# Moving sums, late shared experts and the router's logits in a fused cross-attention and mixture-of-experts kernel

## The chip, the cores and the metric

The kernel runs on one core of a Trainium2 chip. The core has TensorE (PE in the profile, with its weight loads as PEld), VectorE (DVE), ScalarE (ACT), GpSimd (POOL) and SyncE (SP), and 16 DMA engines that all queues share. Each engine executes its instructions in the order in which the program issued them. The metric is device time in microseconds (us); less is better. Matmul results land in PSUM, of which this kernel uses two banks for attention scores and six that everything else takes in turn.

## The reference, cut to what matters

```python
# x (64, 128, 128), ctx_768 (64, 77, 96), all float32; 16 heads of 64
x = x + xattn(layernorm(x), ctx_768, w_q, w_kv, w_out, b_out)
# mixture of experts on h = layernorm(x), 8192 tokens of width 128
logits = h @ router_w.T                    # 8 experts
idx    = top_k(softmax(logits), 2)         # the two best
gate   = logits at idx                     # weighted by the logits themselves
for e in range(8):
    moe += gate[:, e] * ((silu(h @ w1[e].T) * (h @ w3[e].T)) @ w2[e].T)   # inner width 176
moe += (silu(h @ sw1.T) * (h @ sw3.T)) @ sw2.T                             # shared expert
x = x + moe
```

## The kernel before, in words

**Attention.** The 64 batches are 16 groups of four. A group has eight units (batch `b`, half of the heads `t`), so there are 128 units. In the loop at L1099 one unit issues, in this order: the scores of the unit two ahead (`ps`, L365, then on DVE the maximum L374 and the subtraction L376), every second unit the output product of a batch (`py`, L444), the steps of plan slot 2k, the transposes of its own weights (`pa`, L434, copied by ACT at L437), the exponentials of the unit two ahead (ACT, L380), the value products (`pv`, L417, copied by ACT at L422), the steps of plan slot 2k+1, and the weights of the unit two ahead (DVE sum L387 and reciprocal L389, POOL products L395 to L399). The score tile `ps` has one buffer, so the next unit's scores wait until DVE's L376 has read the last ones.

**The plan.** `at(when, step)` writes an order by hand: slot `when` is half a unit, group `g` of attention begins at slot 16g. Slot k always carries one step of `keys` (`pk` L348, copied by ACT at L355) as its first step. After group `g` of attention ends, its routing runs at slots p = 16(g+1) onwards: statistics at p, normalising at p+1, transpose at p+3, logits at p+4 (four matmuls of 8 columns, `pl` L553, then DVE L557 to L561 and ACT's Exp L562), the first choice at p+5 (`choose`, L578 to L572), the second at p+6, `place` at p+8, eight scatters by POOL (`send`, L643) from p+9. The shared expert has its two wide products at p+11 (`gated`), its rest (the inner columns 128 to 175, `gated_rest`: product L654, ACT tanh L518, DVE L520 and L521) at p+12 and its down product at p+14. Attention's own statistics for the next group are at slot 16g+2.

**Experts.** Groups are routed in three sets of 9, 5 and 2. When a set is placed, `tables` works out which expert each block of 128 rows belongs to. Four blocks are a `Quad`: load (SP, L746), copy of weights (ACT and DVE, L769), transpose L775, `first` and `rest` (L782), `down` (L794, L795), ACT's scaling to `y` (L801), and four scatters by POOL (`answer`, L805). The quads of set 0 and two of set 1 run inside attention. `Combine` brings a group's answers back: SP loads the parked sum (L835) and the answers `ya` (L838, 512 KB), DVE adds twice (L847), SP stores (L851).

**The ending.** After attention, `ending` runs passes over 19 jobs: ten quads of set 1 (KEPT), three shared experts (LATE: groups 13, 14, 15), six quads of set 2. In pass k it issues the load of job k+2, the steps listed under k in `ahead_of`, then first(k), transpose(k+1), rest(k), down(k-1), answer(k-1). The jobs stand in the order five quads, three shared experts, eleven quads. The sums of set 0 are all in the plan, from slot 239 to 259, and so partly behind attention's last slot 255 but ahead of the ending, which is at slot 260.

Of the kernel before, what the change touches and what calls it, by code (L numbers as in the profile page):

```python
# [8 lines left out]
F32 = mybir.dt.float32  # L9
# [6 lines left out]
B, NQ, D = 64, 128, 128  # L16
# [9 lines left out]
NT = 10  # L26
# [4 lines left out]
W1, W3, WR, W2F, W2R, WALL = 0, 128, 256, 256 + HI, 384 + HI, 512 + HI  # L31
G = 4
# [4 lines left out]
LATE = 3  # L37

# [17 lines left out]
NAT = 2  # L56
NHR = 2
# [9 lines left out]
def xattn_moe_kernel(  # L67
# [12 lines left out]
    rwT: bass.AP,  # L80
# [72 lines left out]
    rw_sb = const.tile([D, E], F32, name="rw_sb")  # L153
# [4 lines left out]
    nc.sync.dma_start(out=rw_sb, in_=rwT)  # L158
# [33 lines left out]

    hrs = [const.tile([128, T], F32, name=f"hr_{i}") for i in range(NHR)]

# [86 lines left out]
    class Norm:  # L281
# [5 lines left out]
        def stats(self):  # L287
            st = small.tile([128, G, 6], F32, tag="st", name=f"st_{self.name}")
            self.mv = small.tile([128, G, 2], F32, tag="mv", name=f"mv_{self.name}")
# [4 lines left out]
            ve = small.tile([128, G], F32, tag="ve", name=f"ve_{self.name}")  # L294
            nc.vector.tensor_scalar(ve, self.mv[:, :, 1], EPS, None, ALU.add)
            self.rs = small.tile([128, G], F32, tag="rs", name=f"rs_{self.name}")
# [189 lines left out]
    def gated(name, up, silu=False, n=T):  # L486
# [6 lines left out]
        h = ffn.tile([128, T], F32, tag="h", name=f"h_{name}", bufs=3)  # L493
# [12 lines left out]
    def gated_rest(name, up, silu=False, n=T):  # L506
# [4 lines left out]
        hr = hrs[hr_no[0] % NHR]  # L511
        hr_no[0] += 1
# [11 lines left out]
    class Router:  # L524
# [25 lines left out]
        def logits(self):  # L550
            pl = bank(f"pl_{self.g}")
            for b in range(G):
                nc.tensor.matmul(  # L553
                    pl[:, b * E : (b + 1) * E], self.x2T[:, b * NQ : (b + 1) * NQ], rw_sb, start=True, stop=True
                )
            self.lg = lg = self.t3("lg")
            nc.vector.tensor_copy(lg.rearrange("p b e -> p (b e)"), pl[:, : G * E])  # L557
# [37 lines left out]
        def place(self):  # L595
# [22 lines left out]
            for src, to, by in ((at, pos, 1.0), (self.lg, self.pay[:, :, :, D + 1].rearrange("p c b -> p c b"), 0.5)):  # L618
                m = small.tile([128, 2, G, E], F32, tag="picked", name=f"picked_{g}", bufs=2)
# [39 lines left out]
        def shared_rest(self, silu=False):  # L659
            self.hr = gated_rest(f"s{self.g}", self.up, silu)  # L660
# [72 lines left out]
    class Quad:  # L733
# [56 lines left out]
        def down(self):  # L790
# [8 lines left out]
            self.y = ffn.tile([128, QUAD, D], F32, tag="y", name=f"y_{self.name}")  # L799
# [102 lines left out]
    for g in range(NG):  # L902
# [4 lines left out]
        if g + 1 < NG:  # L907
# [3 lines left out]
            at(p + 2, lambda g=g: stats(g + 1))  # L911
# [21 lines left out]
    for g in range(NG - 1):  # L933
        p = 16 * (g + 1)
        routing(g, p, (0, "stats"), (1, "normed"), (3, "transpose"), (4, "logits"), (5, "choose"), (6, "choose_second"))
    for st in sets:
        for g in range(st.start, min(st.start + st.n, NG - 1)):
            p = 16 * (g + 1)
            routing(g, p, (8, "place"))
            if g < NG - LATE:  # L940
                routing(g, p, (11, "shared_up"), (12, "shared_rest"), (14, "shared_down"), (17, "park"))
# [12 lines left out]
    for st, after in zip(sets, sets[1:]):  # L954
# [25 lines left out]
    def job_of(quad, n):  # L980
# [15 lines left out]
    def shared(g):  # L996
# [8 lines left out]

    late = [shared(g) for g in range(NG - LATE, NG)]
    sent_by = KEPT // 2
    jobs = blocks[:sent_by] + late + blocks[sent_by:]
    passes = len(jobs)

    first_of_last = KEPT + LATE
# [19 lines left out]
    for j in range(before_last.n):  # L1031
        c = Combine(before_last, j)
        k = first_of_last + 2 + j
# [163 lines left out]
```

## Time and profile before

| what | value |
|---|---|
| time, median of 3 runs | 988.45 us (987.61 to 989.02) |
| the profiled execution: its own time | 985.48 us |
| the profiled execution: span of the profile | 983.8 us |
| granted TensorE clock, mean | 0.978 |
| PE busy | 924.1 us (94%) |
| PEld, DVE, ACT, POOL busy | 771.5, 671.4, 652.8, 517.4 us |
| HBM read, written | 48.18 MB, 36.33 MB |

The span is what the profile covers; the execution's own time is 1.7 us more. Attention without quads runs from about 20 to 465 us, attention with quads to about 851 us, the ending to 984 us. Busy time is an average over these stages, so the stages are read one by one.

### The profile page before, as it was taken

To read this page: it belongs to the slowest core of one execution; us is meant where nothing else is said; L and a number is where in the kernel's file an instruction comes from. 1 tells how busy PE (TensorE), PEld (TensorE's weight loads), DVE (VectorE), ACT (ScalarE), POOL (GpSimd) and SP (SyncE) were. 2 spreads that over 40 slices of the span, in tenths; PEclk is the share of its full clock that TensorE was granted. 3 is DMA by queue.
4 is the path that set the end of the run, shared out by engine and by line. 5 is a ranking of instruction groups with operands and counts; after the bars stand their busy time and mean duration, and the time that the engine had idled before them with its cause. 6 is when DMAs were issued, how large, how long until landed. Compare 5 with 4: busy or idle time off the path is not lost.

```text
span 983.8 us, 18867 instructions
## 1 busy us (share of the span) xinstructions
PE 924.1 (94%) x6123; PEld 771.5 (78%) x6123; DVE 671.4 (68%) x1751; ACT 652.8 (66%) x1420; POOL 517.4 (53%) x688
## 2 busy tenths in 40 slices
PE   8999999999999999999999999999999987779990
PEld 7887877787787878777888788888888876678980
DVE  4566776676667767768687677776676779566642
ACT  5776767676767667675776767667767665556760
POOL 3244563636364544636367375574474564437673
PEclk9999999999999999999999999999999999879996
DMA  6222212212222222122322221223121135723475
GB/s 179 70 62 71 67 41 81 68 57 71 72 71 65 75 73 65 44 86 80 89 70 76 83 82 55 59 69 99 57 85 49 37 121 169 228 66 98 109 212 174
DMA packets 80882, 85.76 MB, mean 87 GB/s; under 512 B 11328, under 2 KB 62912, under 8 KB 80784
## 3 DMA queue, kind: packets, MB, share of 16 engines
q1 hardware_dynamic: 65920, 56.09, 20.8%
q0 software_dynamic: 8864, 18.30, 5.6%
q10 hardware_dynamic: 6000, 10.16, 2.9%
q8 instruction: 49, 0.80, 0.3%
q14 instruction: 49, 0.40, 0.1%
HBM read 48.18 MB, written 36.33 MB: 86 GB/s over the span
## 4 chain that ended last, share of the span: by engine, by line
PE 69%; DVE 10%; ACT 9%; DMA 5%; issue 4%; SPq 2%; POOL 1%; ACTq 0%; DVEq 0%; POOLq 0%
PE py L444 13%; PE ps L365 11%; PE pk L348 11%; PE pv L417 8%; PE pa L434 5%; PE p L782 4%; PE p_s L654 3%; PE pn L454 2%; PE ph L782 2%; PE pq L794 2%; PE pq L795 2%; DMA answers<-y,to 2%; PE pf L667 1%; PE pf L666 1%; DMA out_dram<-yx 1%
## 5 line engine op out<-in xcount | busy, mean ns | idle before, releaser
L348 PEld LDWEIGHTS pk<-cT,wkq_sb 96*128 96x128 f32 x1024 | 157.8, 189 | 70.0 <-issue 42.8
L805 POOL DMA_INDIRECT answers<-y,to x149 | 146.4, 983 | 89.7 <-issue 44.7
L355 ACT COPY kx<-pk 128x308 f32<-128x308 f32 x256 | 104.5, 417 | 128.5 <-PE pk L348 123.2
L348 PE MATMUL pk<-cT,wkq_sb 96*128 96x154 f32 x1024 | 175.0, 294 | 1.0 <-ACT wkq_sb L265 0.7
L444 PEld LDWEIGHTS py<-vo,aT 128*128 128x128 f32 x1280 | 155.7, 194 | 15.8 <-ACT vo L422 5.2
L365 PE MATMUL ps<-kx,xgT 128*128 128x308 f32 x512 | 156.8, 426 | 9.7 <-DVE sc L376 9.1
L444 PE MATMUL py<-vo,aT 128*128 128x128 f32 x1280 | 157.9, 278 | 4.3 <-ACT vo L422 3.9
L643 POOL DMA_INDIRECT sent<-pay,row x128 | 126.3, 987 | 61.5 <-DVE part L633 27.6
L397 POOL TENSOR_TENSOR at<-sc,ri 128x512 f32<-128x512 f32 x64 | 67.2, 1050 | 170.9 <-DVE ri L389 117.6
L422 ACT COPY vo<-pv 64x512 f32<-64x512 f32 x256 | 147.3, 575 | 2.1 <-ACT vn L462 0.4
L417 PE MATMUL pv<-wvo_sb,cM 96*128 96x512 f32 x256 | 131.1, 594 | 1.0 <-DVE hr L521 0.8
L387 DVE TENSOR_REDUCE sm<-sc 128x8 f32<-128x616 f32 x128 | 101.1, 790 | 39.6 <-ACT sc L380 38.8
L380 ACT ACTIVATE sc<-sc,rs_a 128x616 f32<-128x616 f32 x128 | 105.0, 820 | 26.9 <-DVE sc L376 17.9
L365 PEld LDWEIGHTS ps<-kx,xgT 128*128 128x128 f32 x512 | 88.9, 189 | 38.6 <-issue 9.4
L437 ACT COPY aT<-pa 128x512 f32<-128x512 f32 (+1 forms) x256 | 96.2, 430 | 33.9 <-PE pa L434 29.2
L395 POOL TENSOR_TENSOR at<-sc,ri 128x256 f32<-128x256 f32 x128 | 77.1, 625 | 79.1 <-DVE ri L389 25.3
L376 DVE TENSOR_TENSOR sc<-ps,mx 128x616 f32<-128x616 f32 x128 | 102.4, 800 | 12.5 <-POOL at L399 0.4
L374 DVE TENSOR_REDUCE mx<-ps 128x8 f32<-128x616 f32 x128 | 98.3, 768 | 7.6 <-PE ps L365 6.4
L434 PE MATMUL pa<-ident,at 128*128 128x128 f32 x640 | 92.2, 275 | 0.0
L782 PE MATMUL p<-xT,w 128*128 128x128 f32 x596 | 77.0, 284 | 10.8 <-ACT xT L777 5.5
L434 PEld LDWEIGHTS pa<-ident,at 128*128 128x128 f32 x640 | 75.7, 143 | 11.2 <-issue 10.7
L782 PEld LDWEIGHTS p<-xT,w 128*128 128x128 f32 x596 | 72.8, 198 | 14.6 <-ACT xT L777 8.0
(152 smaller groups left out, 1405.6 us busy)
## 6 DMA issues: line engine op xcount, KB each, us to landing
xb<-sent SPq DMA_DIRECT2D x149, 65.0 KB
last_values<-vn ACTq DMA_DIRECT2D x32, 256.0 KB
vo<-last_values SPq DMA_DIRECT2D x64, 128.0 KB
ya<-answers SPq DMA_DIRECT2D x15, 512.0 KB
xgT<-in_xT_dram SPq DMA_DIRECT2D x16, 256.0 KB
xg<-in_x_dram SPq DMA_DIRECT2D x16, 256.0 KB
parked<-x SPq DMA_DIRECT2D x14, 256.0 KB
yx<-parked SPq DMA_DIRECT2D x14, 256.0 KB
```

The lines of the kernel that those rows point to most:

```text
L348: nc.tensor.matmul(pk[:, k].rearrange("p (b k) -> p b k", k=NKV), wkq_sb[:, 2 * i + k, :], self.cT[:, 2 * p : 2 * (p + 1), :], start=True, ...
L355: nc.scalar.copy(self.kx[p][:, hs, :], pk)
L365: nc.tensor.matmul(ps[:, r, : 4 * NKV].rearrange("p (j k) -> p j k", k=NKV), self.xgT[:, ts], self.kx[p][:, h : h + 4, ks], start=True, st ...
L376: nc.vector.tensor_tensor(at, sc, over_keys(mx), ALU.subtract)
L380: nc.scalar.activation(at, at, AF.Exp, scale=self.norm.rs[:, b : b + 1])
L417: nc.tensor.matmul(pv, self.cM[:, p, KM * r : KM * (r + 2)], wvo_sb[:, h : h + 4, :], start=True, stop=True)
L422: nc.scalar.copy(self.vo[b][rows, 4 * t : 4 * (t + 1), :], pv[rows].rearrange("p (m d) -> p m d", d=D))
L434: nc.tensor.transpose(pa[:, j * NQ : (j + 1) * NQ], keys[:, c : c + 128], ident)
L444: nc.tensor.matmul(py[:, :D], aT[:, m, :], vo[:, m, :], start=(m == 0), stop=(m == NT - 1))
L643: ins = nc.gpsimd.indirect_dma_start(out=sent[st.i], out_offset=bass.IndirectOffsetOnAxis(ap=self.row[:, i : i + 1], axis=0), in_=self.pay ...
L782: nc.tensor.matmul(to[:m, ts], self.w[j][:, c : c + m], self.xT[:, ts], start=True, stop=True)
L805: ins = nc.gpsimd.indirect_dma_start(out=answers[st.i], out_offset=bass.IndirectOffsetOnAxis(ap=self.to[:, j : j + 1], axis=0), in_=self.y ...
```

## The change

Five things change. (1) For groups below 13, the router's weights are packed into eight spare columns of the shared expert's rest weights. The rest product moves from slot p+12 to p+4 and gives the logits as rows 48 to 55 of its result; ACT copies the result from PSUM (`lT`), and at p+5, ahead of `choose`, four transposes bring the logits into the shape in which the old product left them. The separate router matmuls remain for groups 13 to 15. (2) Attention's statistics move from slot 16g+2 to 16g-3. (3) Of set 0's nine sums, three stay in the plan, five slots apart; six move into the ending's passes 7 to 14. (4) In the ending two of the three late shared experts stand last, behind all quads; the last group's routing begins earlier; the last set's sums follow sooner. (5) Within a pass, down(k-1) and answer(k-1) come ahead of rest(k); every second quad writes `y` into attention's `aT` tile, so that there are four buffers of `y` instead of two.

```diff
+WG = WR + IR
+SUMS = 3
-    nc.sync.dma_start(out=rw_sb, in_=rwT)
-    hrs = [const.tile([128, T], F32, name=f"hr_{i}") for i in range(NHR)]
+    hrs = [const.tile([128, T], F32, name=f"hr_{i}") for i in range(NHR + 1)]
...
-        h = ffn.tile([128, T], F32, tag="h", name=f"h_{name}", bufs=3)
+        h = ffn.tile([128, T], F32, tag="h", name=f"h_{name}", bufs=2)
...
         def logits(self):
-            pl = bank(f"pl_{self.g}")
+            pl = bank(f"pl_{self.g}")[:, : G * E].rearrange("p (b e) -> p b e", e=E)
             for b in range(G):
                 nc.tensor.matmul(
-                    pl[:, b * E : (b + 1) * E], self.x2T[:, b * NQ : (b + 1) * NQ], rw_sb, start=True, stop=True
+                    pl[:, b, :], self.x2T[:, b * NQ : (b + 1) * NQ], wsh_sb[:, WG : WG + E], start=True, stop=True
                 )
+            self.weigh(pl)
+
+        def logits_of_rest(self):
+            pl = bank(f"pl_{self.g}").rearrange("p (b e) -> p b e", b=G)
+            for b in range(G):
+                nc.tensor.transpose(pl[:, b, :HI], self.lT[:HI, b * NQ : (b + 1) * NQ], ident[:HI, :HI])
+            self.weigh(pl[:, :, IR : IR + E])
+
+        def weigh(self, pl):
             self.lg = lg = self.t3("lg")
-            nc.vector.tensor_copy(lg.rearrange("p b e -> p (b e)"), pl[:, : G * E])
+            nc.vector.tensor_copy(lg, pl)
...
         def shared_rest(self, silu=False):
-            self.hr = gated_rest(f"s{self.g}", self.up, silu)
+            def up(to, c, m):
+                self.up(to, c, m)
+                if not silu:
+                    self.lT = ffn.tile([128, T], F32, tag="u", name=f"lT_{self.g}")
+                    nc.scalar.copy(self.lT[:HI], to[:HI])
+
+            self.hr = gated_rest(f"s{self.g}", up, silu, hr=None if silu else hrs[NHR])
...
-            at(p + 2, lambda g=g: stats(g + 1))
+            at(p - 3 if g else 2, lambda g=g: stats(g + 1))
...
-        routing(g, p, (0, "stats"), (1, "normed"), (3, "transpose"), (4, "logits"), (5, "choose"), (6, "choose_second"))
+        routing(g, p, (0, "stats"), (1, "normed"), (3, "transpose"))
+        if g < NG - LATE:
+            routing(g, p, (4, "shared_rest"), (5, "logits_of_rest"))
+        else:
+            routing(g, p, (4, "logits"))
+        routing(g, p, (5, "choose"), (6, "choose_second"))
...
-                routing(g, p, (11, "shared_up"), (12, "shared_rest"), (14, "shared_down"), (17, "park"))
+                routing(g, p, (11, "shared_up"), (14, "shared_down"), (17, "park"))
...
-            for j in range(st.n):
+            for j in range(SUMS):
                 c = Combine(st, j)
-                at(p + 7 + 2 * j, c.load)
-                at(p + 10 + 2 * j, c.add)
-                at(p + 11 + 2 * j, c.store)
+                at(p + 7 + 5 * j, c.load)
+                at(p + 10 + 5 * j, c.add)
+                at(p + 11 + 5 * j, c.store)
...
+        if n % 2:
+            job["down"] = lambda: quad.down(bat.tile([128, NT, NQ], F32, tag="aT", name=f"y_{quad.name}")[:, :QUAD, :])
...
-    jobs = blocks[:sent_by] + late + blocks[sent_by:]
+    jobs = blocks[:KEPT] + late[:-2] + blocks[KEPT:] + late[-2:]
...
-        0: [last("stats")],
-        1: [last("normed")],
-        2: [last("transpose"), last("logits")],
-        3: [last("choose")],
-        4: [last("choose_second")],
-        5: [last("place")],
-        6: [last("send", c, b) for b in range(G) for c in range(2)],
-        9: [lambda: tables(last_set)],
+        0: [last("normed")],
+        1: [last("transpose")],
+        2: [last("logits")],
+        3: [last("choose"), last("choose_second")],
+        4: [last("place")],
+        5: [last("send", c, b) for b in range(G) for c in range(2)],
+        7: [lambda: tables(last_set)],
...
-    for j in range(before_last.n):
-        c = Combine(before_last, j)
-        k = first_of_last + 2 + j
+    sums = [(SUMS + 1 + j, Combine(sets[0], j)) for j in range(SUMS, sets[0].n)]
+    sums += [(KEPT + LATE + j, Combine(before_last, j)) for j in range(before_last.n)]
+    for k, c in sums:
         ahead(k, lambda c=c: c.load(ended=True))
+    for k, c in sums:
         ahead(k + 2, c.add)
         ahead(k + 2, c.store)
...
-        ahead(passes + 1, c.load)
-        ahead(passes + 3 + j, c.add)
-        ahead(passes + 3 + j, c.store)
+        ahead(passes, c.load)
+        ahead(passes + 1, c.add)
+        ahead(passes + 1, c.store)
...
-            do(k, "rest")
             do(k - 1, "down")
             do(k - 1, "answer")
+            do(k, "rest")
...
-    at(end + 4, ending)
+    at(end, last("stats"))
+    at(end + 3, ending)
```

More of the change, by code (lines that the diff above doesn't have):

```diff
@@ L79, in xattn_moe_kernel @@
     b_out: bass.AP,
-    rwT: bass.AP,
     wx: bass.AP,
@@ L152, in xattn_moe_kernel @@
     bo_sb = const.tile([128, D], F32, name="bo_sb")
-    rw_sb = const.tile([D, E], F32, name="rw_sb")
     wsh_sb = const.tile([128, WALL], F32, name="wsh_sb")
@@ L287, in stats @@
         def stats(self):
-            st = small.tile([128, G, 6], F32, tag="st", name=f"st_{self.name}")
-            self.mv = small.tile([128, G, 2], F32, tag="mv", name=f"mv_{self.name}")
+            st = small.tile([128, G, 6], F32, tag="st", name=f"st_{self.name}", bufs=4)
+            self.mv = small.tile([128, G, 2], F32, tag="mv", name=f"mv_{self.name}", bufs=4)
             for b in range(G):
@@ L293, in stats @@
                 nc.vector.bn_aggr(self.mv[:, b, :], st[:, b, :])
-            ve = small.tile([128, G], F32, tag="ve", name=f"ve_{self.name}")
+            ve = small.tile([128, G], F32, tag="ve", name=f"ve_{self.name}", bufs=4)
             nc.vector.tensor_scalar(ve, self.mv[:, :, 1], EPS, None, ALU.add)
-            self.rs = small.tile([128, G], F32, tag="rs", name=f"rs_{self.name}")
+            self.rs = small.tile([128, G], F32, tag="rs", name=f"rs_{self.name}", bufs=4)
             nc.gpsimd.tensor_tensor(self.rs, ve, mhalf, ALU.pow)
@@ L504, in gated, with gated_rest @@
         return h
-    def gated_rest(name, up, silu=False, n=T):
+    def gated_rest(name, up, silu=False, n=T, hr=None):
         pr = bank(f"ph_{name}")
@@ L510, in gated_rest @@
         a = ffn.tile([128, T], F32, tag="a", name=f"ar_{name}")
-        hr = hrs[hr_no[0] % NHR]
-        hr_no[0] += 1
+        if hr is None:
+            hr = hrs[hr_no[0] % NHR]
+            hr_no[0] += 1
         of = slice(0, n)
@@ L618, in place @@
             for src, to, by in ((at, pos, 1.0), (self.lg, self.pay[:, :, :, D + 1].rearrange("p c b -> p c b"), 0.5)):
-                m = small.tile([128, 2, G, E], F32, tag="picked", name=f"picked_{g}", bufs=2)
+                m = small.tile([128, 2, G, E], F32, tag="picked", name=f"picked_{g}", bufs=1)
                 for k in range(2):
@@ L788, in rest, with down @@
             self.hr = gated_rest(self.name, self.up, silu, self.n * 128)
-        def down(self):
+        def down(self, room=None):
             py = bank(f"pq_{self.name}")
@@ L798, in down @@
             nc.vector.tensor_tensor(self.to[:, :n], self.xb[:, :n, D], block_row[:, first : first + n], ALU.max)
-            self.y = ffn.tile([128, QUAD, D], F32, tag="y", name=f"y_{self.name}")
+            self.y = ffn.tile([128, QUAD, D], F32, tag="y", name=f"y_{self.name}") if room is None else room
             for j in range(n):
@@ L1006, in xattn_moe_kernel @@
     late = [shared(g) for g in range(NG - LATE, NG)]
-    sent_by = KEPT // 2
-    jobs = blocks[:sent_by] + late + blocks[sent_by:]
+    jobs = blocks[:KEPT] + late[:-2] + blocks[KEPT:] + late[-2:]
     passes = len(jobs)
-    first_of_last = KEPT + LATE
     ahead_of = {
-        0: [last("stats")],
-        1: [last("normed")],
-        2: [last("transpose"), last("logits")],
-        3: [last("choose")],
-        4: [last("choose_second")],
-        5: [last("place")],
-        6: [last("send", c, b) for b in range(G) for c in range(2)],
-        9: [lambda: tables(last_set)],
+        0: [last("normed")],
[5 more added lines that the diff above has]
+        7: [lambda: tables(last_set)],
     }
@@ L1150, in packed @@
         return w
+    shared = packed(a["L0_ffn_sw1"], a["L0_ffn_sw3"], a["L0_ffn_sw2"])
+    shared[:, WG : WG + E] = a["L0_ffn_router_w"].T
     keys = a["ctx_768"].transpose(2, 0, 1)
@@ L1173, in _laid_out @@
         "b_out": a["L0_xattn_b_out"],
-        "rwT": a["L0_ffn_router_w"].T,
         "wx": np.concatenate([packed(w1[e], w3[e], w2[e]) for e in range(E)]),
-        "wsh": packed(a["L0_ffn_sw1"], a["L0_ffn_sw3"], a["L0_ffn_sw2"]),
+        "wsh": shared,
     }
```

## The prediction

> **What bounds the kernel now.** I read first the busy time by stage.
>
> ```profile
> core 0: us, PE busy (x) PEld busy (x) DVE busy (x) ACT busy (x) POOL busy (x), PEclk, DMA share, GB/s
> 100.00:200.00 100.00, 99.86 (x620) 80.20 (x618) 70.99 (x192) 69.09 (x148) 52.14 (x71) 1.00 0.23 68
> 825.00:850.00 25.00, 19.83 (x117) 16.95 (x117) 19.33 (x44) 11.54 (x23) 13.33 (x17) 0.81 0.60 184
> 850.00:875.00 25.00, 15.68 (x114) 15.05 (x113) 13.42 (x36) 11.40 (x26) 5.27 (x6) 0.80 0.47 136
> 925.00:950.00 25.00, 24.85 (x225) 24.61 (x224) 12.53 (x25) 18.40 (x42) 19.19 (x20) 1.00 0.55 152
> 950.00:984.00 34.00, 8.35 (x71) 7.77 (x69) 11.01 (x19) 6.62 (x20) 16.42 (x17) 0.71 0.67 199
> ```
>
> Up to 465 us PE is never idle: there every us added to PE's order is lost for good. Around attention's end (825 to 875) PE is idle for 14 us and clocked low, and the last 34 us hold 8 us of PE work. Those two holes are what parts 3 to 5 of the change aim at.
>
> Then the timeline of the unit in which a group is routed (slots p+4, p+5), DVE and PE lines only, here at 296 to 307 us.
>
> ```profile
> 300.32 0.96 PE L553 MATMUL pl<-rw_sb,x2T_f 128*128 128x8 f32 x8
> 301.13 0.74 PE L434 MATMUL pa<-ident,at 128*128 128x128 f32 x5
> 301.31 0.19 DVE L557 COPY lg<-pl 128x32 f32<-128x32 f32 x1 [1.03 <-PE pl L553]
> 302.25 0.19 DVE L578 TENSOR_REDUCE gs<-gsc 128x4 f32<-128x32 f32 x1 [0.30 <-ACT gsc L562]
> 304.14 0.79 DVE L387 TENSOR_REDUCE sm<-sc 128x8 f32<-128x616 f32 x1
> 305.93 0.80 DVE L376 TENSOR_TENSOR sc<-ps,mx 128x616 f32<-128x616 f32 x1
> 306.88 1.28 PE L365 MATMUL ps<-kx,xgT 128*128 128x308 f32 x4
> ```
>
> DVE's L376 ends at 306.73 and the next scores, which need its buffer, start at 306.88. There is no slack: 0.14 us in each even group of attention, 0.74 in each odd one, all through 75 to 445 us. DVE sets this one unit of every group, though it is only 71% busy.
>
> Last, the end: POOL's timeline, and then the chain of waits behind it.
>
> ```profile
> 874.85 1.03 POOL L805 DMA_INDIRECT answers<-y,to  x1 [11.51 <-issue]
> 970.34 0.96 POOL L805 DMA_INDIRECT answers<-y,to  x1 [0.30 <-issue]
> ```
>
> ```profile
> 970.34 2.23 DMA answers<-y,to
> 972.59 5.01 DMA ya<-answers
> 977.62 0.70 DVE x L847
> ```
>
> From 917 us POOL issues a scatter every 1.26 us without a break, to 971.3; PE's last product ended at 960.6. POOL, not PE, sets the end, and a tail of 12.5 us follows it.
>
> **The logits from the rest (parts 1 and 2): PE's own work.** For 13 groups the 0.81 us of L553 (300.32 to 301.13) goes and four transposes come. The nearest row is `pa`: five in 0.55 us (301.13 to the next product), so 0.44 for four. The rest product (0.86) only moves. Net -0.37 a group, -4.8 us in all. The Trainium skill (TensorE: Matmul & The Clock Gate, Part 4, PE-mode transpose) gives about 275 ns for one transpose in a kernel; the trace has that as its mean duration too (275 ns), but starts are 0.11 us apart. Counted as in the rule, four cost 1.1 us and PE would gain nothing; I take the spacing.
>
> **The same, in order of time.** In the unit above, from PE's 300.32: rest product to 301.18; ACT starts 0.20 after it (as 322.74 to 322.94 in the old place), copies `lT` (nearest row: a 512-wide PSUM copy, 0.59, next start 0.50 later), then tanh, done 302.5. DVE, idle until then, does L520 and L521 at 0.72 each, to 303.9, then L557 to L561, to 304.6. ACT's Exp now stands behind the two `aT` copies, the exponentials, two `vo` copies and a `kx` copy of that unit (from the spacings: 302.4, 303.0, 303.7, 304.9), so it ends at 305.5. From L578 to L387 DVE takes 1.89, from L387 to the end of L376 2.59: 310.0. Scores at 310.15 instead of 306.88. Queued behind DVE's wait are exactly that sum and that subtraction; behind them PE's scores. PE itself is ready at 307.1, so it idles 3.0 us. Loss 3.27, less the 0.86 no longer at p+12: +2.4. Odd groups carry a value product of 0.86 at p+4 and at p+6, which gives PE more to do: idle 2.3, net +2.0. Groups 0 to 8: 4 x 2.4 + 5 x 2.0 = **+19.5** (14 to 23).
>
> Moving attention's statistics (1.5 us of DVE, a 1.0 us power on POOL) away from p+2 doesn't help this: the sum at 297.27 waits for ACT's exponential, not for DVE. At slot 13 they take the place of L520 and L521, so I cost them at nothing; that slot's next scores have 1.9 us of slack, and without it they would cost up to 1.5 a group. The dropped 4 KB load and one more 0.5 us memset lie before POOL's first 5.5 us wait: nothing.
>
> Groups 9 to 12 run among quads. The slack at the same place is 0.21, 1.49, 2.45 and 4.91 us, and ACT, which now waits 1.4 to 2.8 us for DVE ahead of Exp, is free of that wait, so DVE's delay shrinks to 1 or 2 us. I take **+1** (-3 to +6).
>
> **The clock.** Two gaps of this size stand in PE's timeline, and what followed in a table of 5 us stretches (clock in the third column from the right):
>
> ```profile
> 823.28 1.48 PE L365 MATMUL ps<-kx,xgT 128*128 128x308 f32 x4 [2.21 <-DVE sc L376]
> 873.45 1.06 PE L553 MATMUL pl<-rw_sb,x2T_f 128*128 128x8 f32 x8 [2.44 <-ACT x2T_f L318]
> ```
>
> ```profile
> 825.00:830.00 5.00, 5.00 (x31) 4.50 (x31) 4.72 (x13) 1.06 (x4) 2.06 (x3) 0.73 0.23 66
> 875.00:880.00 5.00, 5.00 (x33) 5.00 (x32) 1.75 (x4) 4.30 (x7) 4.02 (x4) 0.66 0.34 93
> ```
>
> After them the clock is 0.73 and 0.66 for 5 us: 1.35 and 1.7 us lost. A gap of 1.65 us at 462 left it at 1.00. The same page of the skill (Part 1, the HAM clock gate) lets the clock fall only after an idle window of about 3.4 us; by that rule nine stalls of 2.3 to 3.0 cost nothing, by the trace up to 1.7 each, 15. I take half the trace's: **+7** (0 to 15).
>
> **The ending (parts 3 to 5).** A sum costs DVE 1.42 us. Four of them leave the stretch before 851, and SP no longer stands at stores (L851) waiting for adds while the load of the quad at slot 252 is queued behind (that quad held DVE up for 3.9 us at 841 to 845). `place` of group 14 comes some 2.8 earlier; POOL's eight sends (1.27 each) and two weight products (1.9 each) then bring the last weights to 840.7 (before: 843.2), and PE's last transposes aren't behind the quad's products any more, which ended at 846.3. Attention ends near 843.5 instead of 850.7.
>
> From there to POOL's first answer of the ending it takes 24.2 us now (850.7 to 874.85), with PE idle for 1.6, 5.3 and 2.4 us; the 5.3 are DVE waiting for a sum's answers before it copies weights. Afterwards the chain is: down of the last attention quad and its `y` 2.9, normalising 1.65, four weight copies on ACT 2.7, tanh and two more on ACT 1.5, DVE to `hr` 2.8, down 1.8, `y`: about 13.9. First answer at 857.4.
>
> POOL then has 62 answers and 8 sends: 70 x 1.263 = 88.4 us; I add 3 for a start and for scatters that take 1.3 under load: 948.8 (before: 96.5 us, with three pauses of 1.9, 1.9 and 3.6 where the late shared experts gave it nothing). With the 12.5 of tail: 961.3. PE's sum is 16 passes of 4.88 and 3 of 4.4, 91.3, from about 844.5 with some 7 of stalls and the last group's routing: 945, and the two shared experts hide POOL's lag instead of following each other ahead of it. So POOL still sets the end. With four buffers of `y`, ACT may run three passes ahead of POOL; the lag after the sends is two.
>
> Down ahead of rest leaves 2.2 us of PE work (first, transpose) between rest(k) and down(k); ACT and DVE need about 2.0 for it: hidden, and POOL's 5.05 a pass covers 0.17. If not, it costs 0.3 a pass, 5 in all. The last group's choices (3.5 us of DVE in one pass), sends and tables come one or two passes earlier, the tables with eight small writes by SP (5.5 us at 784): at most 1 us of PE, among the stalls above, since quads are loaded two passes ahead. Six sums more in passes 7 to 14, each three DMAs on SP's queue, are 1 MB each, on top of about 0.5 MB of quads: 1.5 MB in 4.9 us is 310 GB/s, what the trace reached at 950 to 955 with DMA 97% busy. So it just fits. SP loads a quad two passes ahead (9.8 us) and the landings there grew only from 2.6 to 4.5. Together **-22** (-12 to -30).
>
> **Sum.** 19.5 + 1 + 7 - 22 = +5.5 on the span of 983.8; the profiled execution's own time would be 991.0. It lay 3.0 below the median of the runs, so I forecast **994.0**. A difference under 0.2% (2 us) can't be told from none.
>
> **Rivals.** *The delay is absorbed* (not slower): if DVE's chain costs PE nothing, as happens when Exp isn't late and scores have slack, -4.8 and -22 remain, 962. For it: DVE is idle for 29% there. Against: the 0.14 us. It decides at 2.2 us of stall saved per group; half a stall without clock loss gives 976.
> *The clock stays full*, as the skill's rule has it, and the ending is as worked out or somewhat better: 987 down to 980.
> *DMA saturates in passes 7 to 17*: adds wait for `ya`, weights wait for DVE, PE stalls as at 857 to 863; the ending's gain halves: 1005. For it: 97%; against: PE stayed full at 940 to 955.
>
> **How the numbers follow.** Worked case 0.58 (within it 0.05 faster, 0.08 same, 0.45 slower), absorbed 0.12, full clock 0.15 (0.13 faster, 0.02 same), saturated 0.15. Faster 0.30, same 0.10, slower 0.60. The worked case alone reaches 982 to 1006; with saturation on top and half of the absorbed case below, 976 to 1010.
>
> **What would show it.** Right: the scores after the choosing unit idle 2 to 3 us behind L376 in groups 0 to 8, period of two groups 94 us instead of 89.7, PE under 96 of 100 us between 100 and 400, clock below 1.00 there; attention ends 7 us earlier relative to slot 240, and from POOL's first answer of the ending to its last it takes 91 us. Wrong: no such waits by 445 us, or POOL's last answer long before PE's last product.

## The result and the profile after

| | before | after |
|---|---|---|
| time, median of 4 runs each, taken side by side | 988.71 us | 1002.29 us (1001.77 to 1002.73) |
| span of the profile | 983.8 us | 1001.0 us |
| the profiled execution: its own time | 985.48 us | 1002.73 us |
| granted TensorE clock, mean | 0.978 | 0.978 |

The ratio is 1.0144, with a 95% interval of 1.0129 to 1.0159: slower by 13.6 us. The forecast had 994.0, slower by 5.5. The sign was right, and so was the account of attention; the gain of the ending was half of what the sum had.

Twelve of the eighteen experiments fell on occasions when every kernel was slowed, the kernel before to 1035 to 1046 us, so times are compared by the ratio to the kernel before, run beside them on the same chip, and where that kernel's time is given below as 1035 us or more, sizes don't carry over. The lines of `before.py` have moved: L365 is now L366, L376 L377, L387 L388, L518 to L521 L520 to L523, L557 L570, L562 L575, L805 L824.

The stages first, as before: the window, busy us of PE, PEld, DVE, ACT and POOL (with instructions), then clock, DMA share and GB/s.

```profile
100.00:200.00 100.00, 94.88 (x575) 75.87 (x574) 70.11 (x188) 64.69 (x139) 49.34 (x69) 0.98 0.21 62
870.00:895.00 25.00, 21.58 (x176) 21.02 (x175) 15.08 (x38) 16.02 (x36) 11.73 (x13) 0.93 0.29 73
930.00:940.00 10.00, 3.64 (x22) 3.45 (x21) 3.54 (x7) 1.98 (x4) 7.76 (x8) 0.81 0.87 306
950.00:975.00 25.00, 24.60 (x213) 23.51 (x212) 16.81 (x31) 16.10 (x36) 19.21 (x20) 1.00 0.92 264
975.00:1001.00 26.00, 12.32 (x72) 8.65 (x70) 12.73 (x21) 4.88 (x12) 9.46 (x10) 0.80 0.73 229
```

Where PE was never idle (99.86 of 100) it now loses 5 us in each 100, at a clock of 0.98. The hole at attention's end is smaller (PE is idle for 8.4 of the 50 us from 853 to 903, against 14.5 of the 50 from 825 to 875 before), and a new one stands at 930 to 940. The product matrix `ps` names what ends the first loss:

```profile
its engine sat idle before it (us, times) until:
  DVE grest L603: 22.5, 9
  DVE sc L377: 10.4, 9
```

Nine stalls, one in the routing of each of groups 0 to 8, 2.5 us each on average. L603 is put down as their end because it is the DVE instruction next to it; the one that frees the scores' buffer is L377 just ahead. Here is the unit that the prediction worked through (then at 296 to 307 us), on PE, ACT and DVE in order of time:

```profile
315.45 1.02 PE L667 MATMUL ph_s<-x2T_f,wsh_sb 128*112 128x512 f32 x2
316.51 0.59 ACT L677 COPY lT<-ph_s 112x512 f32<-112x512 f32 x1 [0.44 <-PE ph_s L667]
...
318.24 0.55 PE L565 MATMUL pl<-ident,lT 112*128 112x112 f32 x4
318.33 0.69 DVE L523 TENSOR_TENSOR hr<-ur_s,ph_s 48x512 f32<-48x512 f32 x1
319.05 0.19 DVE L570 COPY lg<-pl 128x32 f32<-128x32 f32 x1
...
320.34 0.23 ACT L575 ACTIVATE gsc<-gsc 128x32 f32<-128x32 f32 x1
320.60 0.19 DVE L591 TENSOR_REDUCE gs<-gsc 128x4 f32<-128x32 f32 x1 [0.91 <-ACT gsc L575]
322.49 0.79 DVE L388 TENSOR_REDUCE sm<-sc 128x8 f32<-128x616 f32 x1
324.28 0.80 DVE L377 TENSOR_TENSOR sc<-ps,mx 128x616 f32<-128x616 f32 x1
325.22 1.35 PE L366 MATMUL ps<-kx,xgT 128*128 128x308 f32 x2 [2.91 <-DVE grest L603]
```

DVE reaches the logits at 319.05, behind the rest's own two operations, for which it had waited 2.20 us until ACT's tanh was done; ACT's Exp then stands behind other copies, DVE waits 0.91 us for it, and all that is queued behind (the choosing, the sum L388, the subtraction L377) makes the scores 2.91 us late. Counted from PE's start in this unit (300.32 and 315.45), the logits reach DVE 2.6 us later than before and the subtraction starts 3.2 later: the wait for Exp, 0.91 instead of 0.30, is the smaller part of it. The rest of the way of the prediction, Exp to L388 1.89 and L388 to the end of L377 2.59, is there to the hundredth. The start of the scores against the kernel before grows by 2.82 us in this unit, and by 1.67 more in the next, since the clock falls after the gap:

```profile
320.00:325.00 5.00, 2.31 (x14) 1.60 (x13) 3.98 (x14) 1.58 (x6) 1.32 (x2) 1.00 0.00 0
325.00:330.00 5.00, 4.78 (x22) 4.10 (x23) 3.82 (x12) 2.27 (x4) 1.46 (x3) 0.66 0.01 2
```

By unit 80 (482 us) the scores are 28.2 us later than before, and in the last unit of attention they are 28.5 later, with up to 31.7 in between (all counted with the 0.4 us by which the changed kernel began earlier). What then happens is in POOL's row: the first two pauses of the ending, and the chain behind the last answer.

```profile
890.23 0.96 POOL L824 DMA_INDIRECT answers<-y,to  x1 [6.48 <-ACT y L820]
...
898.76 0.96 POOL L824 DMA_INDIRECT answers<-y,to  x1 [3.62 <-ACT y L820]
...
906.62 0.96 POOL L824 DMA_INDIRECT answers<-y,to  x1 [3.10 <-ACT a L497]
...
986.24 0.96 POOL L824 DMA_INDIRECT answers<-y,to  x1 [0.30 <-ACT ar_s L517]
```

```profile
986.24 2.99 DMA answers<-y,to
989.25 5.50 DMA ya<-answers
```

The first answer of the ending's own jobs goes out at 890.23 (before: 874.85 of 983.8), and from 906.62 on POOL issues without a pause to 987.2. The three late shared experts no longer interrupt it (before, a pause of 3.6 us), but the last group's routing, now packed into passes 0 to 4, makes two pauses of its own.

### The profile page after: what moved, and what is told of

It is laid out like the page before. It is cut to its first block, busy times and chain, and to the rows that moved or that the text cites. A ratio compares the mean times of both kernels' runs of the same rounds, so it can differ in the third digit from the quotient of the medians.

```text
span 1001.0 us, 18788 instructions
## 1 busy us (share of the span) xinstructions
PE 928.5 (93%) x6071; PEld 771.3 (77%) x6071; DVE 685.8 (69%) x1751; ACT 662.1 (66%) x1433; POOL 519.2 (52%) x689
## 4 chain that ended last, share of the span: by engine, by line
PE 64%; DVE 13%; ACT 11%; DMA 6%; issue 3%; SPq 1%; ACTq 1%; POOL 1%; DVEq 0%; POOLq 0%
PE py L445 13%; PE ps L366 11%; PE pk L349 10%; PE pv L418 7%; PE pa L435 4%; PE p L801 4%; PE p_s L667 2%; PE pq L814 2%; PE pn L455 2%; PE pq L813 2%; ACT vo L423 2%; DVE sc L377 2%; DVE sm L388 2%; DVE mx L375 2%; ACT sc L381 2%
## 5 line engine op out<-in xcount | busy, mean ns | idle before, releaser
L366 PE MATMUL ps<-kx,xgT 128*128 128x308 f32 x512 | 161.3, 436 | 33.0 <-DVE grest L603 22.5
L824 POOL DMA_INDIRECT answers<-y,to x149 | 147.7, 991 | 82.7 <-ACT y L820 26.6
L445 PEld LDWEIGHTS py<-vo,aT 128*128 128x128 f32 x1280 | 159.5, 198 | 15.8 <-ACT vo L423 4.1
L445 PE MATMUL py<-vo,aT 128*128 128x128 f32 x1280 | 161.2, 281 | 3.4 <-ACT vo L423 2.7
L366 PEld LDWEIGHTS ps<-kx,xgT 128*128 128x128 f32 x512 | 89.9, 192 | 64.2 <-issue 34.4
L388 DVE TENSOR_REDUCE sm<-sc 128x8 f32<-128x616 f32 x128 | 101.0, 789 | 41.3 <-ACT sc L381 40.4
L438 ACT COPY aT<-pa 128x512 f32<-128x512 f32 (+1 forms) x256 | 96.4, 431 | 33.5 <-PE pa L435 28.5
L377 DVE TENSOR_TENSOR sc<-ps,mx 128x616 f32<-128x616 f32 x128 | 102.4, 800 | 13.2 <-POOL at L398 0.5
L435 PEld LDWEIGHTS pa<-ident,at 128*128 128x128 f32 x640 | 75.4, 141 | 11.4 <-issue 10.7
L801 PE MATMUL p<-xT,w 128*128 128x128 f32 x596 | 74.2, 278 | 6.3 <-ACT xT L796 6.3
L801 PEld LDWEIGHTS p<-xT,w 128*128 128x128 f32 x596 | 70.3, 193 | 9.5 <-ACT xT L796 8.2
```

Source lines behind the costliest of these rows:

```text
L366: nc.tensor.matmul(ps[:, r, : 4 * NKV].rearrange("p (j k) -> p j k", k=NKV), self.xgT[:, ts], self.kx[p][:, h : h + 4, ks], start=True, st ...
L377: nc.vector.tensor_tensor(at, sc, over_keys(mx), ALU.subtract)
L388: nc.vector.tensor_reduce(sm, at, AX.X, ALU.add)
L435: nc.tensor.transpose(pa[:, j * NQ : (j + 1) * NQ], keys[:, c : c + 128], ident)
L445: nc.tensor.matmul(py[:, :D], aT[:, m, :], vo[:, m, :], start=(m == 0), stop=(m == NT - 1))
L801: nc.tensor.matmul(to[:m, ts], self.w[j][:, c : c + m], self.xT[:, ts], start=True, stop=True)
```

## The experiments

### Which part costs what: the ending alone, the logits alone

*ending only*: after, with the old logits, the rest back at p+12 and the statistics at p+2 (the packed weights and the spare tile stay). *logits only*: the kernel before with parts 1 and 2.

```diff
-            routing(g, p, (4, "shared_rest"), (5, "logits_of_rest"))
+            routing(g, p, (4, "logits"))                    # e1: for every group
...
+        routing(g, p, ..., (12, "shared_rest"), ...)        # e1
+            at(p + 2, lambda g=g: stats(g + 1))             # e1
...
+    jobs = blocks[:sent_by] + late + blocks[sent_by:]       # e2: sums, jobs and passes as before
```

> The changed kernel with parts 1 and 2 undone: logits by the router's own four matmuls at p+4, the rest product back at p+12, attention's statistics back at slot 16g+2. Theory (the loss lies wholly in parts 1 and 2, the ending gains about 11.5 as read from the trace): 988.7 - 11.8 = 977 us, the scores after the choosing unit wait no more than 0.3 us on average in groups 0 to 8, clock 1.00 between 100 and 400 us. Rival (the ending is worth the 22 of the forecast and parts 1 and 2 cost more than 28, for instance because a shifted attention part spoils the ending): 966 to 969.

> The kernel before with parts 1 and 2 alone: logits out of the rest product and statistics half a group earlier, the sums and the ending as they were. Theory (each part costs what the trace shows, no interaction): 988.7 + 28 = 1016 to 1018 us, of which 22 to 25 is stall behind the subtraction on VectorE and the lower clock after it in groups 0 to 8, all of it there by 455 us. Rival (the ending hides or returns a part of it): 1005 to 1012, with the difference to the kernel before shrinking between 830 us and the end.

The ending alone: 976.11 us, ratio 0.9889 (0.9872 to 0.9905), a gain of 11.3. The logits alone: 1015.13, ratio 1.0271 (1.0254 to 1.0288), a loss of 27.7. Together +16.4, where the change has +13.6; the intervals are 1.7 us to each side, so the two parts add up within about 3 us and nothing large passes between them. The rival that had the ending at -22 is out. The ending alone also beats both kernels; it is the version to keep.

In the ending alone the stage 100 to 200 us is what it was before the change:

```profile
100.00:200.00 100.00, 99.86 (x619) 80.22 (x618) 71.06 (x192) 68.80 (x148) 52.01 (x71) 1.00 0.22 68
```

### The choices one slot later

```diff
-        routing(g, p, (5, "choose"), (6, "choose_second"))
+        routing(g, p, (6, "choose"), (7, "choose_second"))
```

> The changed kernel with the two choices one slot later (p+6 and p+7 instead of p+5 and p+6), so that ScalarE has delivered the exponential long before VectorE reaches the choosing, and the choosing lies behind the row sum of another unit. Theory (VectorE's in-order wait for the late Exp is the cost): the scores' stalls of 2.9 and 2.2 us shrink to under 0.7, the clock stays at 1.00 between 100 and 400, and the time is 970 to 977 us. Rival (the cost is the added work itself, the copy on ScalarE, the four transposes and the two VectorE operations moved to p+4, wherever the choices stand): 995 to 1002, with the stall merely moved by one slot.

979.86 us, ratio 0.9909 (0.9889 to 0.9929), against 1.0144 for the change: 23 us, of the 25 between the change and the ending alone (0.9889), are gone, and the copy `lT`, the transposes and the early rest are all still there. The same unit, at 305 to 308 us:

```profile
304.81 0.19 DVE L574 TENSOR_TENSOR gsc<-lg,gm 128x32 f32<-128x32 f32 x1
304.92 0.79 DVE L388 TENSOR_REDUCE sm<-sc 128x8 f32<-128x616 f32 x1
306.71 0.80 DVE L377 TENSOR_TENSOR sc<-ps,mx 128x616 f32<-128x616 f32 x1
307.43 0.17 DVE L591 TENSOR_REDUCE gs<-gsc 128x4 f32<-128x32 f32 x1
307.66 1.28 PE L366 MATMUL ps<-kx,xgT 128*128 128x308 f32 x4
```

DVE goes straight on to L388 and L377 and does the choosing behind them, when Exp is long done; the scores don't wait. This shows that the cost lies in what stands ahead of the subtraction in DVE's queue, and not in the added work. It doesn't tell the wait for Exp (0.91 us) from the choosing itself (1.89), since both moved. The time is 3 us above the theory's range: against the ending alone the scores are 2.0 us later at 438 us (0.4 of it a later start of the whole) and 1.7 more at 530. Of that 1.7, 1.4 came at 470 us, where the clock is at half for 6.8 us, in the ending alone for 3.4; the rest are small steps that I didn't follow up. So the added work is nearly free, but it doesn't pay either: 979.86 is 3.8 above the ending alone by the medians, 2 by the ratios.

### The clock: filling the gap

```diff
+        if g < SETS[0]:
+            at(p + 7, lambda: warm(8))    # eight 128x128 products, results unused
```

> The changed kernel with eight dummy products of 128x128 (about 1.8 us of TensorE, results unused) at slot p+7 in groups 0 to 8, so that TensorE is busy for most of the time in which it waits for the choosing unit. Theory (about 8 of the 28 us are a lower clock after gaps of 2.9 us, 4 x 1.65 + 1.7): the gap falls to about 1.1 us, the clock stays at 1.00 between 100 and 400, and the time falls by 6 to 9, to 993 to 996 us. Rival (the lower clock comes from something else, or the dummies merely add to TensorE's work): 1002 to 1018 us with the same losses of 1.65 us after each even group.

993.68 us, ratio 1.0057 (1.0040 to 1.0074): 8.6 less than the change, with *more* work on PE. The dummies lie in the gap, which falls to 1.12 us, and the next stretch stays at full clock:

```profile
317.08 1.95 PE L274 MATMUL pi<-ident 128*128 128x128 f32 x16
320.16 1.02 PE L366 MATMUL ps<-kx,xgT 128*128 128x308 f32 x3 [1.12 <-DVE grest L603]
```

```profile
320.00:325.00 5.00, 4.84 (x39) 4.49 (x40) 4.40 (x17) 2.85 (x6) 1.39 (x2) 1.00 0.00 2
```

The stall's end (L377) is where it was, so the 8.6 us are the clock's share of the loss: the sum over the nine gaps read from the trace of after is 8.5 (four gaps of 2.91 us at 1.5 to 1.7 each, the first of 2.18 at 1.71, four of 2.17 at 0.07).

### What sets the end of the ending: more for POOL, more for PE

```diff
+    ahead(13, lambda: [nc.gpsimd.memset(hrs[NHR], 0.0) for _ in range(8)])   # POOL; tile not used there
+    ahead(13, lambda: warm(16))                                              # PE, a kernel of its own
```

> The ending alone with eight more GpSimd instructions (about 4 us) in pass 13. Where the kernel before takes about 987 us, theory (GpSimd's row of answers sets the end): 0.9889 of it plus 4 us, ratio 0.992 to 0.994. Rival (another engine or the DMAs set the end): ratio 0.988 to 0.990. Where it takes 1035 us and more, the ratio says little, as in the run before (0.9878 against 0.9836).

The ending alone with POOL's eight memsets: 980.96 us, ratio 0.9924 (0.9899 to 0.9949), against 0.9889 (0.9872 to 0.9905) for the ending alone: +3.5 us, though the two intervals overlap slightly. In POOL's row the answer behind the memsets starts 6.00 us after the one ahead, instead of 1.26:

```profile
936.60 0.96 POOL L824 DMA_INDIRECT answers<-y,to  x1 [0.30 <-issue]
937.56 4.82 POOL L1065 MEMSET hr<- 128x512 f32 x8
942.60 1.31 POOL L824 DMA_INDIRECT answers<-y,to  x1 [0.22 <-issue]
```

4.7 us more stand in POOL's row at that place. In the traces the row from the ending's first answer to its last grows from 98.4 to 102.5 us, nothing else in it changes by as much, and the tail behind it stays at 12.1: POOL sets the end. The kernel with more for POOL, one with more for PE and their base were also run where the kernel before took 1035.4 us, and there they told nothing apart:

> The ending alone (parts 1 and 2 undone) once more, as the base for the three runs beside it on the same chip: ratio to the kernel before 0.986 to 0.990 if the chip is like that of the first runs, 0.980 to 0.986 if it is like the two others.

> The ending alone with eight more GpSimd instructions (memsets of an unused 128x512 tile, about 4 us in all) in pass 13, where GpSimd has answers queued. Theory (GpSimd's row of answers sets the end): the base plus 3.5 to 4.5 us. Rival (another engine or the DMAs set the end): the base within 1 us.

> The ending alone with sixteen dummy products of 128x128 on TensorE (about 3.6 us) in pass 13. Theory (TensorE runs ahead of GpSimd by what eight sends have put into GpSimd's queue, and the stall of 6.4 us in pass 11 has used most of it up, 1 to 2 us being left): the base plus 1.5 to 3. Rival 1 (TensorE has slack of 4 us or more): the base within 0.5 us. Rival 2 (no slack): plus 3.6 and more.

Base 0.9836 (0.9803 to 0.9869), POOL 0.9878 (0.9847 to 0.9910), PE 0.9874 (0.9843 to 0.9905): the intervals overlap. How much PE could lose before it sets the end is open, and it can't be much: in the ending alone PE's last product ends at 958.7 and POOL's last answer at 960.4, where before the change they lay 10.7 us apart (960.6 and 971.3); in the change itself PE's last product even ends 1.6 us behind POOL's last answer.

### Smoothing the first passes

*smooth*: weights are copied first in each pass, the choices stand in passes 3 and 4. *quick start*: the last group's normalising and second copy go to POOL, and weights are copied one pass ahead instead of two.

```diff
-        3: [last("choose"), last("choose_second")],
+        3: [last("choose")],
+        4: [last("choose_second")],                     # smooth: place, sends, tables one pass later
...
+                    nc.gpsimd.tensor_scalar(to[:, b, :], ...)              # quick start, last group only
-            ahead(max(k - 2, 0), job["weights"])
+            ahead_of.setdefault(k - 1, []).insert(0, job["weights"])       # quick start
```

> The ending alone (parts 1 and 2 undone) with the work that made GpSimd pause in passes 2 and 3 spread: each pass copies weights before the last group's routing steps, and the two choices stand in passes 3 and 4, with place, sends and tables one pass later. Theory (the pauses of 3.5 and 2.8 us in passes 2 and 3 are on the path, and TensorE, which ends level with GpSimd, gains as well since group 15's sends come no later): 970 to 972 us against 976.1, GpSimd's time from its first answer of the ending to its last 91 to 93 instead of 97.5. Rival (TensorE with its stall of 6.4 us for the first quad of the last set is as late as GpSimd, and that stall stays or grows with the sends a pass later): 975 to 979, TensorE's last product behind GpSimd's last answer.

> The ending alone with weights copied first in each pass and the two choices in passes 3 and 4, once more, since in the first run the chip's engines stalled from 500 us on in every kernel, the one before too (1046 us). What that run left: GpSimd's early pauses were 5.4, 1.9, 1.4 and 3.2 us instead of 6.2, 3.5 and 2.8, no shorter in sum. Theory now (the early passes are paced by TensorE, ScalarE and VectorE together, and a pause pushed out of one pass comes back in the next): 974 to 977 us. Rival (the pauses were on the path and the spread removes them): 970 to 972.

> The ending alone with less for ScalarE in the first passes: the last group's normalising and its second copy go to GpSimd, which is idle there, and each quad's weights are copied one pass ahead of their use instead of two. Theory (the late first answer and the pauses are ScalarE's extra work in passes 0 to 3, and GpSimd's row shifts as a whole): GpSimd's pause ahead of its first answer 3 to 4 us instead of 6.2, the pause in pass 2 under 2.5 us instead of 3.5, and the base minus 3 to 5. Rival (TensorE's stall for the first quad of the last set has no more cover then, so the end doesn't move): the base within 1 us, with TensorE's last product 2 us or more behind GpSimd's last answer.

> The ending alone with the last group's normalising and second copy on GpSimd and each quad's weights copied one pass ahead of use instead of two. In the disturbed run GpSimd's first pauses fell from 6.2, 3.5 and 2.8 to 4.7 (with two copies of its own ahead of it), 2.4 and 2.1, and the time didn't fall. Where the kernel before takes about 987 us, theory (those pauses are on the path): ratio 0.984 to 0.987. Rival (TensorE's stall for the first quad of the last set takes over): ratio 0.988 to 0.991.

Smooth: 0.9801 (0.9735 to 0.9867) and 0.9846 (0.9824 to 0.9869), beside a kernel before of 1045.8 and 1035.5 us, against 0.9836 of the base beside one of 1035.4: no gain seen. Quick start: 0.9885 beside 1035.4, and 0.9905 (0.9880 to 0.9931) beside 987.9, against 0.9889 of the ending alone: no gain either, though the two pauses fell from 3.6 and 3.1 us to these:

```profile
871.46 0.96 POOL L829 DMA_INDIRECT answers<-y,to  x1 [2.69 <-ACT y L825]
...
878.70 1.03 POOL L829 DMA_INDIRECT answers<-y,to  x1 [2.37 <-ACT w L793]
```

What I had not costed is the place of the normalising in POOL's queue, behind four answers. PE's transposes of the last group wait for it, and they stand ahead of the second job's products:

```profile
853.95 2.16 POOL L307 TENSOR_SCALAR pay<-x,rs_f,shift_f 128x128 f32<-128x128 f32 x4
854.87 1.77 PE L322 MATMUL pxT_f<-ident,pay 128*128 128x128 f32 x4 [3.98 <-POOL pay L307]
```

So the first answer came 35.2 us after attention's last scores instead of 30.9, and what the pauses gave was lost ahead of them. PE's last product (962.4) also fell 1.3 us behind POOL's last answer (961.1). The experiment moved the loss instead of removing it; it doesn't tell what the pauses alone are worth.

### Undoing parts 3, 4 and 5 of the ending one at a time

```diff
+    jobs = blocks[: KEPT // 2] + late + blocks[KEPT // 2 :]   # old jobs: with the old passes of the last group and last sums
+            do(k, "rest"); do(k - 1, "down"); do(k - 1, "answer")         # old pass: and two buffers of y
+            for j in range(st.n): ... at(p + 7 + 2 * j, c.load) ...       # old sums: all nine in the plan
```

> The ending alone with part 4 undone: the three late shared experts in the middle, the last group's routing and the last sums where they were before. Parts 3 and 5 stay. Theory (part 4 brings most of the ending's 11.3 us, since it removes GpSimd's pauses around the shared experts and the two empty stretches at the start): 983 to 986 us, pauses of 1.9, 1.9 and 3.6 us back in GpSimd's answers. Rival (parts 3 and 5 bring most, the sums out of the way before attention's end): 977 to 980.

> The ending alone with part 4 undone, once more for the same reason. Theory (part 4 is worth most of the ending's gain): 983 to 986 us, one pause of over 3 us in GpSimd's row where the three shared experts follow each other. Rival (part 4 is worth little, the pauses only move): 977 to 980.

> The ending alone with part 5 undone: the rest product ahead of the down product and two buffers of y. Theory (GpSimd sets the end, its answers come every 1.263 us whichever order the pass has, so this part is worth little): 976 to 978 us. Rival (down products 0.9 us earlier in each pass let GpSimd start sooner, and four buffers let it run without pauses): 980 to 984, with pauses in GpSimd's row after 880 us.

> The ending alone with part 5 undone, once more for the same reason; there it was level with the version that has part 5. Theory (GpSimd's answers set the end, the order within a pass is worth nothing): 975 to 977.5 us. Rival: 980 to 984.

> The ending alone with part 3 undone: all nine sums of the first set in the plan, two slots apart. Theory (the six sums hold up vector work before attention's end and the copy of weights behind it, worth the 4.5 us by which attention ends earlier and a part of the start): 981 to 984 us, attention's last output product 4 us later. Rival (the sums cost as much in the passes 7 to 14, where the DMA is 95% busy, as they cost in the plan): 975 to 978.

> The ending alone with part 3 undone, once more for the same reason; there attention's last output product and GpSimd's first answer of the ending came later than with part 3 (first pause 11.8 us instead of 5.4 to 7.6). Theory (sums in the plan hold up the copies of weights behind attention's end): 981 to 985 us, attention's last output product 2 to 4 us later and GpSimd's first long pause 11 to 12 us instead of 6.2. Rival: 975 to 978.

All six stand beside a kernel before of 1045.8 or 1035.5 us; only the order and the waits are read from them.

| undone | ratio, first | ratio, second |
|---|---|---|
| nothing (base, another call, before 1035.4) | | 0.9836 (0.9803 to 0.9869) |
| part 5, order in a pass and y buffers | 0.9788 (0.9720 to 0.9856) | 0.9855 (0.9829 to 0.9881) |
| part 4, shared experts last | 0.9905 (0.9869 to 0.9942) | 0.9934 (0.9913 to 0.9955) |
| part 3, six sums behind attention | 0.9933 (0.9911 to 0.9954) | 0.9988 (0.9972 to 1.0003) |

Part 5 is worth nothing that shows. Without part 4 POOL stands for 20 us behind the eight sends, where the three shared experts follow each other (3.6 us in the trace of before; why it is 20 here is open). Without part 3 DVE waits for a sum's answers ahead of the weights that POOL's first answer depends on:

```profile
885.46 1.45 DVE L866 TENSOR_TENSOR yx<-yx,ya 128x512 f32<-128x512 f32 x2 [3.51 <-DMA ya<-answers]
886.91 1.77 DVE L788 COPY w<-wx_sb 128x624 f32 x4
...
899.94 0.96 POOL L824 DMA_INDIRECT answers<-y,to  x1 [12.71 <-ACT y L820]
```

The last batch's output product starts 18.1 us after attention's last scores, against 13.7 with part 3 (the base, before at 1035.4), and the first answer comes 43.8 after them, against 31.1. So part 3 brings nearly all of the earlier first answer: with the kernel before at 987 us it came 45.0 after the last scores, and with the change's ending 30.9. That is where the ending's gain comes from.

## Why the prediction was right or wrong

**The logits' chain, +19.5.** Right. The shift of the scores by unit 80 is 28.2 us; less the 8.5 of clock it is 19.7. Stalls of 2.91 us (even groups of attention) and 2.17 (odd ones) stand where 3.0 and 2.3 were forecast, and moving the choices from ahead of the subtraction took the loss away.

**Groups 9 to 12, +1.** Near in number, +0.3 from unit 80 to the last, but by luck: the scores first fell 3.4 us further behind, 1.6 of it at 491 to 498 us by the clock, and then won 3.2 back among the quads. The delay of 1 or 2 us a group that the prediction had there wasn't seen as such.

**The clock, +7.** Right in kind and near in size: 8.5 in the trace, 8.6 by filling the gaps. The size was luck: the prediction took half of 15 as a hedge, and five of the nine gaps cost 1.5 to 1.7 us because of where they fell (last section). The rival in which the clock stays full is out: the idle window of about 3.4 us that the Trainium skill gives (TensorE: Matmul & The Clock Gate, Part 1, HAM clock gate) need not be idle throughout, since gaps of 2.91 us were enough here four times, and one of 2.18.

**Moved statistics, dropped load, memset at nothing.** Right as far as the trace of after goes up to 445 us: from group to group the scores' lag changes where the rest product came in and went away, in the choosing unit and by the clock behind it, and nowhere else by more than 0.1 us.

**The ending, -22.** This is the step that failed: the ending alone gave -11.3. Its parts, in the trace of the ending alone, counted from attention's last scores, against the kernel before:
- Attention's end and the first answer: 30.9 instead of 45.0, a gain of 14.2; the forecast had 857.4 for the first answer, 27.6 after those scores, a gain of 17.4. It is 3.2 us short: the last matmul of attention's output products started 15.8 us after those scores, where the forecast had attention's end at 13.7, and from there to the first answer it took 15.1 instead of 13.9.
- POOL's row, first to last answer: forecast 91.4 to the end of the last one, with 3 us of allowance; measured 98.4 (97.0 in the change), and 96.5 before. This term was mis-sized by 7 us. 6.3 are the two pauses: the first three jobs' answers start 8.5 and 7.9 us apart, where POOL alone would need 5.05. The prediction put all three pauses of before (1.9, 1.9 and 3.6) down to the late shared experts, and so let them go with these. The trace of before doesn't bear that out: the first pause ends at 881.86, ahead of PE's first product of a shared expert, and the second ends at the fourth quad's answers; only the 3.6 are the shared experts'. In POOL's and PE's rows of before:

```profile
881.86 0.96 POOL L805 DMA_INDIRECT answers<-y,to  x1 [1.93 <-ACT y L801]
...
890.43 1.96 PE L654 MATMUL p_s<-x2T_f,wsh_sb 128*128 128x512 f32 x4
...
893.55 0.95 POOL L805 DMA_INDIRECT answers<-y,to  x1 [1.91 <-issue]
...
917.30 0.96 POOL L805 DMA_INDIRECT answers<-y,to  x1 [3.62 <-ACT a L496]
```

  The last group's Exp, a table load ahead of Silu (1.28 us of ACT) and the choices stand in these passes before the change too. With the change two such pauses are 3.6 and 3.1 us long, and POOL has no answers in store in those passes: until the eight sends stand in its queue, a late pass is a pause of POOL. I had cost the earlier routing at "at most 1 us of PE". In the trace of the ending alone both choices now follow each other on DVE (871.83 to 875.39) ahead of a copy of weights; that drawing the routing together made the pauses longer is read from this order and not shown by an experiment, since neither *smooth* nor *quick start* won time.
- The tail: 12.1 (ending alone) and 13.8 (change) instead of 12.5.

Attention's last scores lay 1.3 us later in that profile than in that of before, which makes -14.2 + 2.0 - 0.4 + 1.3 = -11.3.

**POOL sets the end.** Right for the ending alone, and shown by adding to its row; but PE now ends level with it, so what less work for POOL alone would win is not shown. **DMA "just fits".** Half right: at 92% busy PE is full at 950 to 975. But something like the rival's wait did appear in one place. In pass 11 DVE waits for the first quad of the last set, which is loaded from what the last group's sends wrote:

```profile
DVE to L817 <- DMA xb<-sent: 9.0, 1, 9.0
PE pq L814 <- DVE hr L518: 6.6, 2, 6.4
```

PE lost 6.4 us there, in the ending alone too; POOL's row shows no pause at that time, since POOL had the sends and waiting answers to work off, so it cost nothing at the end. Whether the quad came late because of full DMA engines (87% busy at 930 to 940) or because of the sends' place isn't told apart. **Down ahead of rest, hidden.** No difference showed when it was undone, beside a kernel before of 1035 us and more.

**The profiled execution, 3.0 below the median.** I added this to the result. The profile after lies 0.4 above its median, so the spans differ by 17.2 and the medians by 13.6; how far one kernel's profiled execution lies from its median says little about another's.

## What to carry to other kernels

An engine that takes its queue in order passes every wait and every small operation on to all that is queued behind: before moving a short operation to an earlier slot, list what stands behind it on its engine and who waits for that. Where it can go behind the work that others wait for, moving it one slot can give nearly all back (23 of 25 us here). When steps are pulled together to shorten the start of a pipeline, ask whether the engine that sets the end has work in store at that moment; if not, a pass's extra length can be added to the end. And before a pause is counted as won, check in the trace which step it really waits for.

## What the runs showed of the hardware

The clock is not lowered by the length of one gap alone. Gaps of 2.91 us cost 1.5 to 1.7 us in the next 5 us four times out of four; gaps of 2.17 cost 0.07 four times, but the first, of 2.18 at 83 us, cost 1.71; 1.12 cost nothing. The trace of after settles why. In it the clock is lowered to half for 3.41 us at a time, once for 6.83 and once more near the end, and all its changes lie a multiple of 3.41 us apart. Cut into these windows, the first gap of 2.18, one of 2.17 and one of 2.91 look like this (busy us of PE first, clock third from the right):

```profile
82.90:86.31 3.41, 1.23 (x6) 0.82 (x6) 3.13 (x9) 1.19 (x4) 1.39 (x2) 1.00 0.19 71
86.31:89.72 3.41, 3.41 (x16) 3.22 (x15) 2.75 (x6) 1.31 (x3) 1.39 (x2) 0.50 0.00 0
178.47:181.88 3.41, 2.23 (x12) 1.38 (x10) 3.07 (x11) 1.39 (x4) 0.56 (x1) 1.00 0.20 77
181.88:185.29 3.41, 2.42 (x16) 2.16 (x17) 3.13 (x11) 2.27 (x4) 0.84 (x3) 1.00 0.02 5
185.29:188.70 3.41, 3.41 (x27) 2.65 (x27) 2.18 (x7) 1.00 (x2) 1.38 (x2) 1.00 0.01 2
321.83:325.24 3.41, 0.50 (x5) 0.29 (x3) 3.13 (x10) 0.00 (x0) 1.39 (x2) 1.00 0.00 0
325.24:328.65 3.41, 3.41 (x10) 2.71 (x11) 2.92 (x10) 2.27 (x4) 1.02 (x2) 0.50 0.01 2
```

The first gap lies in one window, which is left 36% busy, and the next window has half the clock. The second lies across the edge of two windows, each is still over 60% busy, and nothing follows. In eight traces (before, after, the ending alone, the logits alone, the choices later, the filled gap, and POOL's memsets and *quick start* beside 987.9 us) I counted all such windows: 48 of 51 full-clock windows with PE busy for less than half were followed by one at half clock, 3 of 33 with 50 to 60%, and none with more. The gaps of 2.91 us came 95.8 us apart, which is nearly 28 windows, so each fell in one window almost whole; that all four cost their 1.7 us is a matter of where they fell.

The ending alone has a case of two gaps, of 0.67 and 1.65 us, that lie for the most part in one window and cost 1.45 us together; before the change the 1.65 had cost nothing:

```profile
459.75:463.16 3.41, 1.65 (x6) 0.92 (x6) 3.17 (x6) 0.55 (x2) 1.82 (x3) 1.00 0.66 191
463.16:466.57 3.41, 3.01 (x8) 2.31 (x9) 3.25 (x7) 2.28 (x4) 2.89 (x5) 0.50 0.00 0
```

So idle time within a window counts together. The length fits the free-running window of about 3.4 us that the same page and part of the Trainium skill give for the gate; that a window about half idle is enough is what these traces add. Half the clock for 3.41 us loses 1.7, as measured.
